# Recurrent layer with gated residual: ScalarE and VectorE held in written order for two steps, the kept steps' transfers pinned to fixed steps

## Chip, cores and metric

The kernel runs on one core of a Trainium2 chip. The metric is the device time in microseconds (us) of one execution, as the median of several. Five engines matter: the PE (TensorE, matrix products), DVE (VectorE), ACT (ScalarE), POOL (GpSimd) and SP (SyncE), which does no arithmetic here and issues nearly all transfers (DMAs) from one queue, in order.

## What is computed

Two layers, in float32, for x of shape 64 × 256 × 1024 (batch, time, width) and a condition of shape 64 × 1024. The second layer's transform is undone by its inverse and the gate is the same for all times, so its result is y · (1 + gate); with the residual it is y · (2 + gate).

```python
# layer 0: a recurrence over 256 time steps, with a residual
xW = einsum('ntd,dh->nth', x, Wx) + b
h  = cond
for t in range(256):
    h = tanh(h @ Wh + xW[:, t])
    y[:, t] = x[:, t] + h
# layer 1: a gate from the condition, on all levels of a Haar transform of y
g    = silu(cond @ W1.T + b1)
gate = sigmoid(g @ W2.T + b2)
out  = y + inverse_haar(gate * haar(y))
```

## The kernel before, in words

**Layout.** A step's state is 64 × 1024; on the chip it is a tile of 128 partitions × 512 elements. The time axis is worked on in pairs of steps: `pairs[i]` holds x for steps 2i and 2i + 1 (128 × 1024), and `s` is the step's place in its pair.

**The recurrent product** h @ Wh (`h_product`, L228) is done by Strassen's scheme in seven quarter-size products, in the order 1, 2, 5, 6, 7, 4, 3. Their left sides come from hT by four DVE operations (`strassen_sides`, L210; L213 to L216), their right sides are Wh's quarters and sums t5, t6, t4 and a changed b12, made once at step 0 (`StrassenWeight`, L150; L164 and L175). Product 1 goes to a PSUM bank m16, ACT copies it out (L236), product 6 is added to it in the same bank and copied again (L240); product 6 can start only after the first copy. Products 2, 3 and 4 are added straight to `acc`, a PSUM bank into which ACT has copied xW of this step before (`put`, L222; L225). DVE joins the parts (L242, L245, L249), ACT does the tanh (L428), DVE the transpose (L430).

**The input product** x @ Wx runs on the same PE in the gaps of the recurrence, one pair ahead. For accuracy x and Wx are split in parts (`XWork`, L265): `x_high` (L116), x1 (L273), x2 (L275) on DVE, and x0, a cast of x_high on ACT (L281). Its `first` part (banks "mixed", then half of "main") is issued in odd steps, its `second` part in even ones. The sums are finished by ACT (L289), POOL (L290) and DVE (L321), written to DRAM (`sum_d`, L325) and read back in the layout of the state (`xw`, eight loads, L331).

**The gate** uses the same PE: the product with W1 at step 0 (tiles `w1_k`), then `gate_hidden` (L387: DVE L388, ACT sigmoid L390, DVE L391 and transpose L393, giving g1T); the product with W2, one block after each of the steps 1 to 8; then `gate_factor` (L396), giving `factor` = 2 + gate.

**Output.** POOL adds hT to the pair (L473) and multiplies by factor (L415); SP stores the pair to yT (L497). For the first four pairs the factor isn't known yet: they are "kept" in DRAM (L500), and each of their eight steps is later loaded again into a tile `again` (L516), multiplied (POOL, L519) and stored (L520). `again` has one buffer (tag "spare", which b1's tile used before), so a load has to wait for the store before it.

**Order of the work.** A scheduler orders each engine's instructions by its own estimate of when they can start, except on engines under `manual_schedule`, which keep the order of the program: PE for the whole kernel, DVE from L355 to `in_order.close()` (L451, behind the split of x for pair 2, in step 0). ACT, POOL and SP are ordered by the scheduler throughout. On each engine the instructions then run strictly in the order so fixed.

**Buffers for W1.** The tag "t" (`sums_tile`, L119) has six buffers, used first by blocks 0 to 5 of Wx, then by blocks of W1, then by t5, t6 and t4 (two tiles each). The pool "slabs" has six buffers, used by pairs of x, blocks 6 and 7 of Wx, the other blocks of W1, and W2.

Of the kernel before, what the change touches and what calls it, by code (L numbers as in the profile page):

```python
# [62 lines left out]
B = D // P  # L63
# [4 lines left out]
KB = B // 2  # L68
S = 2
# [10 lines left out]
def tile_cond_resid(  # L80
# [13 lines left out]
    nc = tc.nc  # L94
    const = ctx.enter_context(tc.tile_pool(name="const", bufs=1))
# [11 lines left out]
    def slab(name: str):  # L107
        return slabs.tile([P, D], F32, tag="slab", name=name)
# [10 lines left out]
    def sums_tile(name: str):  # L119
        return wpool.tile([P, D], F32, tag="t", bufs=3 * KB // 2, name=name)  # L120
# [17 lines left out]
    def load_bias(v: bass.AP, pool, tag: str, name: str):  # L138
        t = pool.tile([P, G, F], F32, tag=tag, name=name)
        for q in range(Q):  # L140
            for g in range(G):
                nc.sync.dma_start(out=t[q * R : (q + 1) * R, g, :], in_=v[q : q + 1, :].broadcast_to((R, F)))
        return t[:].rearrange("p g f -> p (g f)")
# [49 lines left out]
    def plain_product(ps, vT, w, k: int, of=None, start: bool = True, stop: bool = True) -> None:  # L193

        for g in range(G):
            col = of(g) if of else (g * B + k) * R
            for q in range(Q):


                nc.tensor.matmul(  # L200
                    out=ps[q * R : (q + 1) * R, g * F : (g + 1) * F],
                    lhsT=vT[:, col : col + R],
                    rhs=w[:, q * F : (q + 1) * F],
                    start=start and k == 0 and g == 0,
                    stop=stop and k == B - 1,
                    skip_group_check=True,
                    tile_position=(0, q * R),
                )

    def strassen_sides(hT, t: int):  # L210
        a11, a12, a21, a22 = (hT[:, i * E : (i + 1) * E] for i in range(4))
        s = sums.tile([P, 4, E], F32, tag="s", name=f"s{t}")
        nc.vector.tensor_sub(s[:, 2], a11, a21)  # L213
        nc.vector.tensor_add(s[:, 0], a21, a22)
        nc.vector.tensor_sub(s[:, 1], s[:, 0], a11)
        nc.vector.tensor_sub(s[:, 3], a12, s[:, 1])  # L216
        return {1: a11, 2: a12, 3: s[:, 3], 4: a22, 5: s[:, 0], 6: s[:, 1], 7: s[:, 2]}
# [4 lines left out]
    def put(xw, t: int):  # L222

        acc = bank("acc", f"acc{t}")
        nc.scalar.copy(acc, flat(xw))  # L225
        return acc
# [25 lines left out]
    def bank(tag: str, name: str):  # L252
        return one_pool.tile([P, HALF], F32, tag=tag, name=name)
# [86 lines left out]
    h0T = const.tile([P, W], F32, tag="h0T", name="h0T")  # L340
# [11 lines left out]

    ctx.enter_context(tc.manual_schedule(engines={mybir.EngineType.PE}))
    in_order = ExitStack()
    in_order.enter_context(tc.manual_schedule(engines={mybir.EngineType.DVE}))  # L355
    now = XWork(1)
    now.begin()
    acc, acc1, gate_ps = bank("acc", "acc0"), bank("m57", "acc1_raw"), bank("gate", "gate_ps1")
# [8 lines left out]
    w1 = []  # L367

    def load_w1(k: int) -> None:
        w1.append(sums_tile(f"w1_{k}") if k <= KB else slab(f"w1_{k}"))  # L370
        nc.sync.dma_start(out=w1[k], in_=w1T[k])

    def split_block(k: int) -> None:
        wx_s.append(split_weight(wx_raw[k], k))

    for k in range(B):
        x_block(k)
        split_block(k) if k < B - 1 else None
        if k in (3, 5):
            now.block(k // 4)  # L380
    for k in range(KB + 2):
        load_w1(k)
    for k in range(B):
        h_block(k)
# [2 lines left out]
    def gate_hidden(z):  # L387
        nc.vector.tensor_add(z, gate_ps, z)  # L388
        s = work.tile([P, W], F32, tag="h", bufs=1, name="s1")
        nc.scalar.activation(s, z, AF.Sigmoid)  # L390
        nc.vector.tensor_mul(s, s, z)  # L391
        g1T = const.tile([P, W], F32, tag="factor", name="g1T")
        nc.vector.transpose(g1T, s)  # L393
        return g1T

    def gate_factor(z):  # L396
        nc.vector.tensor_add(z, gate_ps, z)
        nc.scalar.activation(z, z, AF.Sigmoid)
        factor = const.tile([P, W], F32, tag="factor", name="factor")
        nc.vector.transpose(factor, z)  # L400
        nc.vector.tensor_scalar_add(factor, factor, 2.0)
        return factor

    def blocks(v):
        return v[:].rearrange("p (g b m) -> p g b m", g=G, b=B)
# [15 lines left out]
    kept, again, factor = [], [], None  # L421
    for t in range(T):
        i, s = divmod(t, S)
        if s == 0 and t:
            xw = xw_next
        if t:
            h = h_product(acc, sides, t)
        nc.scalar.activation(h, h, AF.Tanh)  # L428
        hT = work.tile([P, W], F32, tag="hT", name=f"hT{t}")
        nc.vector.transpose(hT, h)  # L430
        if t + 1 < T:
            sides = strassen_sides(hT, t)
        if t == 0:
            acc = bank("acc", "acc1")
            nc.vector.tensor_add(acc, acc1, b_n)
            split_block(B - 1)
            for k in range(KB + 2, B):
                load_w1(k)
            for k in range(2, B):
                if k == B - 1:  # L440
                    plain_product(gate_ps, h0T, w1[0], 0)
                now.block(k)
            now.take_mixed()
            wh_s = StrassenWeight(wh_raw)
            wh_s.first()
            xw_next = now.finish()
            for k in range(1, B):
                plain_product(gate_ps, h0T, w1[k], k)
            wh_s.others()
            later = XWork(2)  # L450
            in_order.close()  # L451


        elif s == 0:
            acc = put(xw[1], t + 1)
            if i + 1 < NP:
                now.second()
                if i + 2 < NP:
                    later = XWork(i + 2)
                xw_next = now.finish()  # L460
        if s == 1 and i + 2 < NP:
            now = later
            now.first()
        if s == 1 and i + 1 < NP:
            acc = put(xw_next[0], t + 1)

        if t == 1:
            g1T = gate_hidden(b1_n)


        x = pairs[i]
        if t + S < T:
            nc.gpsimd.tensor_add(of_step(x, s), of_step(x, s), blocks(hT))  # L473
        if 1 <= t <= B:
            k = t - 1
            if k == 0:
                gate_ps = bank("gate", "gate_ps2")
            w2 = slab(f"w2_{k}")
            nc.sync.dma_start(out=w2, in_=w2T[k])
            plain_product(gate_ps, g1T, w2, k)  # L480
            if k == B - 1:
                factor = gate_factor(load_bias(b2, const, "h0T", "b2_n"))
        if t + S >= T:

            for half in range(2):
                part = slice(half * KB, (half + 1) * KB)
                v = of_step(x, s)[:, :, part]
                nc.vector.tensor_add(v, v, blocks(hT)[:, :, part])
                nc.vector.tensor_mul(v, v, blocks(factor)[:, :, part])
                to = yT[i].rearrange("p (b s n) -> p s b n", b=B, s=S)[:, s, part]  # L490
                (nc.sync, nc.scalar)[half].dma_start(
                    out=to, in_=x[:].rearrange("p (b s n) -> p s b n", b=B, s=S)[:, s, part]
                )
        elif factor is not None:
            scale(x, s)
            if s == S - 1:
                nc.sync.dma_start(out=yT[i], in_=x)  # L497
        elif s == S - 1:
            kept.append(dram.tile([P, D], F32, tag="kept", bufs=B // S, name=f"kept{i}"))
            nc.sync.dma_start(out=kept[i], in_=x)  # L500
        if s == S - 1:
            del pairs[i]
            if i + 3 < NP:
                load_x(i + 3)


        if t >= 2 * B and t % 2 == 0 and kept:

            def at(v):
                return v.rearrange("p (b s n) -> p s b n", b=B, s=S)[:, r]  # L510

            if t % 4 == 0:
                j, r = divmod(t // 4 - B // 2, S)
                again = const.tile([P, W], F32, tag="spare", name=f"again{t}")
                by_block = again[:].rearrange("p (b n) -> p b n", b=B)
                nc.sync.dma_start(out=by_block, in_=at(kept[j]))  # L516
            else:
                v = again[:].rearrange("p (b g m) -> p g b m", b=B, g=G)
                nc.gpsimd.tensor_mul(v, v, blocks(factor))  # L519
                nc.sync.dma_start(out=at(yT[j]), in_=by_block)  # L520
                if (j + 1, r + 1) == (len(kept), S):
                    kept = []
# [28 lines left out]
```

## Time and profile before

| what | value |
|---|---|
| median of 3 runs | 3113.57 us (3110.15 to 3116.41) |
| span of the profiled execution | 3116.2 us, PE clock 0.996 of full |
| PE busy | 3082.5 us of 3116.2 |
| DVE, ACT, POOL busy | 1757.3, 714.8, 1109.0 us |
| PE waits over 0.1 us, 0 to 262 us | 21.2 us in seven waits |
| PE waits over 0.1 us, 250 to 3080 us | 0.4 us in two waits |
| "again" loads (L516), 8 | issued between 72.9 and 232.5 us |
| "again" products (L519), 8 | between 167.7 and 237.7 us |

The page gives busy times over the whole span. The view of waits lists, for one engine, what it waited for, how long in all and how often. The timeline lists instructions by time; neighbours of one kind are merged ("x32"), and what stands in brackets is the idle time of the engine just before and the instruction that ended it. "SPq" rows are DMA issues on SP's queue; their duration is the issue, not the transfer.

### The profile page before, as it was taken

The page shows a single profiled execution, that of the slowest core. Times are in us where ns is not written, and L with a number is a line of the kernel's source. Part 1 is how long each engine was busy: PE and PEld are TensorE (multiplying, and loading weights), DVE is VectorE, ACT ScalarE, POOL GpSimd, SP SyncE. Part 2 cuts the span into 40 slices and gives each one's busy share as a digit, 9 for nine tenths or more (in the row PEclk, how much of TensorE's full clock was granted, in tenths as well). Part 3 has the DMA queues.
Part 4 walks back from the last instruction along what each step waited for, and adds up shares of the span by engine and source line. Part 5 has one row for each costly group of instructions (what it writes and reads, how often), then busy time and mean ns, then how long its engine had stood idle before and what let it go on. Part 6 is the DMA issues. An engine that isn't in the chain of part 4 may idle for free.

```text
span 3116.2 us, 137774 instructions
## 1 busy us (share of the span) xinstructions
PE 3082.5 (99%) x63856; PEld 2697.4 (87%) x63856; DVE 1757.3 (56%) x2732; ACT 714.8 (23%) x1421; POOL 1109.0 (36%) x766
## 2 busy tenths in 40 slices
PE   8999999999999999999999999999999999999998
PEld 5878888888888888888888888888888888888887
DVE  7555555565555555555655555555555555655554
ACT  3222222222222222222222222222222222222221
POOL 1233333333333333333333333333333333333332
PEclk9999999999999999999999999999999999999999
DMA  7343222222222222222222222222222222222222
GB/s 261 124 120 103 85 92 89 94 86 94 94 90 90 90 91 90 91 90 97 84 93 94 91 86 94 91 91 91 89 94 88 92 89 91 90 91 89 97 71 69
DMA packets 161665, 298.85 MB, mean 96 GB/s; under 512 B 42048, under 2 KB 107840, under 8 KB 161088
## 3 DMA queue, kind: packets, MB, share of 16 engines
q1 hardware_dynamic: 159888, 289.50, 27.3%
q8 instruction: 500, 8.19, 1.1%
q14 instruction: 77, 0.63, 0.1%
q10 hardware_dynamic: 1200, 0.52, 0.1%
HBM read 154.14 MB, written 135.79 MB: 93 GB/s over the span
## 4 chain that ended last, share of the span: by engine, by line
PE 95%; DMA 1%; POOL 0%; DVE 0%; SPq 0%; issue 0%; ACT 0%; DVEq 0%; ACTq 0%; POOLq 0%
PE main L257 30%; PE m L183 29%; PE acc L183 21%; PE mixed L257 15%; DMA again<-kept 1%; DMA yT<-again 0%; POOL again L519 0%; PE gate_ps L200 0%; DMA xw<-sum_d 0%; SPq L331 0%; DVE t L164 0%; DMA x<-xT 0%; DVE h L249 0%; ACT h L428 0%; POOL x L415 0%
## 5 line engine op out<-in xcount | busy, mean ns | idle before, releaser
L473 POOL TENSOR_TENSOR x<-x,hT 128x512 f32<-128x512 f32 x254 | 449.8, 1771 | 1729.2 <-DVE hT L430 1711.7
L257 PE MATMUL main<-wx,x 128*128 128x512 f32 x4064 | 981.1, 393 | 0.0
L257 PEld LDWEIGHTS main<-wx,x 128*128 128x128 f32 x4064 | 752.8, 188 | 178.4 <-issue 25.8
L242 DVE TENSOR_TENSOR y<-m,u 128x256 f32<-128x256 f32 x255 | 108.3, 425 | 882.1 <-PE m L183 882.1
L183 PE MATMUL m<-t,s 128*32 128x128 f32 x16320 | 496.8, 274 | 3.4 <-ACT y L236 3.4
L257 PE MATMUL mixed<-wx,x 128*128 128x512 f32 x2032 | 499.0, 397 | 0.0
L183 PEld LDWEIGHTS m<-t,s 128*32 128x32 f32 x16320 | 454.6, 111 | 4.1 <-ACT y L236 3.6
L257 PEld LDWEIGHTS mixed<-wx,x 128*128 128x128 f32 x2032 | 371.6, 188 | 97.8 <-issue 25.0
L290 POOL TENSOR_TENSOR sum<-sum,b_row 128x512 f32<-128x512 f32 x254 | 326.4, 1286 | 213.0 <-ACT sum L289 213.0
L428 ACT ACTIVATE h<-h 128x512 f32<-128x512 f32 x256 | 162.0, 633 | 790.2 <-DVE h L249 789.0
L415 POOL TENSOR_TENSOR x<-x,factor 128x512 f32<-128x512 f32 x246 | 332.0, 1350 | 15.4 <-DMA x<-xT 5.7
L249 DVE TENSOR_TENSOR h<-acc,y 128x512 f32<-128x512 f32 x255 | 176.4, 692 | 236.4 <-PE acc L183 236.4
L430 DVE STREAM_TRANSPOSE hT<-h 128x512 f32<-128x512 f32 x256 | 182.2, 712 | 204.2 <-ACT h L428 204.2
L183 PEld LDWEIGHTS m<-wh,hT 128*32 128x32 f32 x8160 | 209.0, 110 | 92.8 <-issue 85.6
L275 DVE SCALAR_TENSOR_TENSOR x<-x,x_high 128x1024 fp32r<-128x1024 f32 x127 | 283.9, 2235 | 0.1
L183 PE MATMUL m<-wh,hT 128*32 128x128 f32 x8160 | 276.4, 276 | 4.6 <-DVE hT L430 4.6
L183 PE MATMUL acc<-wh,hT 128*32 128x128 f32 x8160 | 272.2, 274 | 7.2 <-ACT acc L225 7.2
L183 PE MATMUL m<-wh,s 128*32 128x128 f32 x8160 | 270.5, 273 | 0.0
L183 PE MATMUL acc<-wh,s 128*32 128x128 f32 x8160 | 270.3, 273 | 0.2 <-issue 0.2
L183 PE MATMUL acc<-t,hT 128*32 128x128 f32 x8160 | 269.5, 273 | 0.0
L281 ACT CAST x<-x_high 128x1024 fp32r<-128x1024 f32 x127 | 132.9, 1046 | 482.4 <-PE main L257 466.2
L183 PEld LDWEIGHTS acc<-wh,hT 128*32 128x32 f32 x8160 | 229.6, 111 | 8.8 <-ACT acc L225 8.7
(52 smaller groups left out, 2309.1 us busy)
## 6 DMA issues: line engine op xcount, KB each, us to landing
x<-xT SPq DMA_DIRECT2D x128, 512.0 KB, 3.7
sum_d<-sum SPq DMA_DIRECT2D x127, 512.0 KB, 3.1
xw<-sum_d SPq DMA_DIRECT2D x1016, 64.0 KB, 2.0
yT<-x SPq DMA_DIRECT2D x123, 512.0 KB, 3.6
wx<-wx SPq DMA_DIRECT2D x8, 512.0 KB, 8.6
wh<-wh SPq DMA_DIRECT2D x8, 512.0 KB, 11.2
w<-w1T SPq DMA_DIRECT2D x8, 512.0 KB, 8.2
w<-w2T SPq DMA_DIRECT2D x8, 512.0 KB, 4.0
```

What stands on the lines that cost most here:

```text
L183: nc.tensor.matmul(out=out[q * R : (q + 1) * R], lhsT=a[:, k * R : (k + 1) * R], rhs=wh_s.sides[i][k][:, q], start=first and k == 0, stop= ...
L242: nc.vector.tensor_add(y[:, 1:3], m57[:, : 2 * E].rearrange("p (i e) -> p i e", i=2), u[:].unsqueeze(1).broadcast_to((P, 2, E)))
L249: nc.vector.tensor_add(h, acc, flat(y))
L257: nc.tensor.matmul(out=acc[h], lhsT=v[:, k * P : (k + 1) * P], rhs=wx_s[k][which][:, h * HALF : (h + 1) * HALF], start=start and k == 0, s ...
L275: nc.vector.scalar_tensor_tensor(out=self.x2, in0=self.x1[:].bitcast(F32), scalar=-UP, in1=self.high, op0=ALU.mult, op1=ALU.add)
L281: nc.scalar.copy(self.x0, self.high)
L290: nc.gpsimd.tensor_add(s, s, b_row[:, h * HALF : (h + 1) * HALF])
L415: nc.gpsimd.tensor_mul(of_step(x, s), of_step(x, s), blocks(factor))
L428: nc.scalar.activation(h, h, AF.Tanh)
L430: nc.vector.transpose(hT, h)
L473: nc.gpsimd.tensor_add(of_step(x, s), of_step(x, s), blocks(hT))
```

## The change

Four edits. ACT joins DVE in keeping the program's order, and both keep it until behind `gate_hidden` in step 1, where it ended for DVE in step 0. The load of b2 is moved to that place from step 8. Of W1, block 5 goes to a buffer of tag "t" in place of a slab, and block 6 is loaded with the first ones; blocks 0 and 1 of the product with W1, where it was block 0 alone, come ahead of the last x block. The eight kept steps are loaded at the ends of steps 19, 27, ..., 75, where it was steps 16, 20, ..., 44, and multiplied at steps 23, 31, ..., 79; `keep_in_program_order` pins each load on SP, and each product on POOL, behind the instruction that the program has just ahead of it on that engine. The stores L520 are not pinned. The purpose is to keep instructions that the scheduler places early or in a bunch from standing ahead of those that the recurrence needs.

```diff
-    in_order.enter_context(tc.manual_schedule(engines={mybir.EngineType.DVE}))
+    in_order.enter_context(tc.manual_schedule(engines={mybir.EngineType.DVE, mybir.EngineType.Activation}))
...
-        w1.append(sums_tile(f"w1_{k}") if k <= KB else slab(f"w1_{k}"))
+        w1.append(sums_tile(f"w1_{k}") if k < 3 * KB // 2 else slab(f"w1_{k}"))
...
-    for k in range(KB + 2):
+    for k in range(B - 1):
         load_w1(k)
...
-            for k in range(KB + 2, B):
-                load_w1(k)
+            load_w1(B - 1)
             for k in range(2, B):
                 if k == B - 1:
-                    plain_product(gate_ps, h0T, w1[0], 0)
+                    for j in range(2):
+                        plain_product(gate_ps, h0T, w1[j], j)
                 now.block(k)
...
-            for k in range(1, B):
+            for k in range(2, B):
                 plain_product(gate_ps, h0T, w1[k], k)
             wh_s.others()
             later = XWork(2)
-            in_order.close()
...
         if t == 1:
             g1T = gate_hidden(b1_n)
+            b2_n = load_bias(b2, const, "h0T", "b2_n")
+            in_order.close()
...
-                factor = gate_factor(load_bias(b2, const, "h0T", "b2_n"))
+                factor = gate_factor(b2_n)
...
-        if t >= 2 * B and t % 2 == 0 and kept:
+        if t >= 2 * B and t % 4 == 3 and kept:
...
-            if t % 4 == 0:
-                j, r = divmod(t // 4 - B // 2, S)
+            if t % 8 == 3:
+                j, r = divmod(t // 8 - B // 4, S)
...
-                nc.sync.dma_start(out=by_block, in_=at(kept[j]))
+                tc.keep_in_program_order(nc.sync.dma_start(out=by_block, in_=at(kept[j])))
...
-                nc.gpsimd.tensor_mul(v, v, blocks(factor))
+                tc.keep_in_program_order(nc.gpsimd.tensor_mul(v, v, blocks(factor)))
```

## The prediction, made before the changed kernel ran

> **What bounds the kernel now.** I read the page first, for the busiest engine:
>
> ```profile
> PE 3082.5 (99%) x63856; PEld 2697.4 (87%) x63856; DVE 1757.3 (56%) x2732; ACT 714.8 (23%) x1421; POOL 1109.0 (36%) x766
> ```
>
> The core has 33.7 us in which the PE is not busy. The change leaves the count of matmuls alone, so it can win back only PE idle time, and the slow matmuls that follow a pause. The view of waits, PE alone, for 0 to 262 us, says where the idle time is:
>
> ```profile
> PE acc L200 <- DMA wx<-wx: 8.0, 1, 8.0
> PE acc L183 <- ACT acc L225: 7.0, 2, 5.2
> PE m L183 <- ACT y L236: 3.4, 1, 3.4
> PE gate_ps L200 <- issue: 2.4, 1, 2.4
> PE gate_ps L200 <- DMA w<-w1T: 0.4, 2, 0.2
> ```
>
> The same view for 250 to 3080 us shows 0.4 us in all: the steady stretch cannot give anything. The 8.0 us at the start (first weights) and about 5 us at the end (the last two steps) lie outside the edits. Four waits are left, in two places.
>
> Place one, steps 12 and 14 (timeline of PE, SP and ACT; columns: start, us, engine, line, operation):
>
> ```profile
> 193.53 0.61 SPq L325 DMA_DIRECT2D sum_d<-sum  x1
> 199.69 0.57 SPq L520 DMA_DIRECT2D yT<-again  x1
> ...
> 204.15 0.59 ACT L225 COPY acc<-xw 128x512 f32<-128x512 f32 x1 [9.77 <-DMA xw<-sum_d]
> ...
> 204.79 1.94 PE L183 MATMUL acc<-wh,hT 128*32 128x128 f32 x32 [5.23 <-ACT acc L225]
> 206.50 3.64 PE L183 MATMUL m<-t,s 128*32 128x128 f32 x64
> ...
> 233.42 1.08 PE L183 MATMUL acc<-wh,hT 128*32 128x128 f32 x32 [1.80 <-ACT acc L225]
> ```
>
> SP starts its DMAs in one queue. DVE finished sum at 187.5 (L321, 186.84 + 0.69), but sum_d goes out at 193.5, because the queue stood in front of L516, a load of "again" that waits until the previous yT<-again has landed; and the xw loads go out at 200.4, because L520 ahead of them waits for the POOL product L519. So acc is late. The distance between the first matmuls of successive steps, from the PE timeline, is 11.91 us undisturbed; here it is 20.14 for step 12 (198.48 to 218.62) and 13.94 for step 14 (230.54 to 244.48). Excess: 8.23 + 2.03 = **10.3 us**.
>
> Place two, step 1:
>
> ```profile
> 55.29 0.69 DVE L116 TENSOR_SCALAR x_high<-x 128x1024 int32<-128x1024 int32 x1
> 56.01 1.04 ACT L281 CAST x<-x_high 128x1024 fp32r<-128x1024 f32 x1 [11.28 <-DVE x_high L116]
> 56.96 0.26 ACT L236 COPY y<-m 128x128 f32<-128x128 f32 x1
> 57.27 1.93 PE L183 MATMUL m<-t,s 128*32 128x128 f32 x32 [3.38 <-ACT y L236]
> 57.27 1.22 DVE L275 SCALAR_TENSOR_TENSOR x<-x,x_high 128x1024 fp32r<-128x1024 f32 x1
> ...
> 67.66 1.38 DVE L216 TENSOR_TENSOR s<-hT,s 128x128 f32<-128x128 f32 x1
> 68.97 0.68 DVE L391 TENSOR_TENSOR s<-s,b_n 128x512 f32<-128x512 f32 x1
> 69.68 0.71 DVE L393 STREAM_TRANSPOSE g1T<-s 128x512 f32<-128x512 f32 x1
> 70.49 1.89 PE L200 MATMUL gate_ps<-w,g1T 128*32 128x256 f32 x16 [2.38 <-issue]
> ```
>
> The copy of m16 (L236), ready to run at about 52, is queued on ACT behind a cast that waits for DVE. Later the PE waits for g1T, last in DVE's queue. Step 1 with its gate part takes 20.99 us (51.09 to 72.08) and step 2 13.76, where such a step takes 12.82: excess 8.17 + 0.94 = 9.1 us.
>
> [...] after the 5.23 us wait 64 matmuls take 3.64 us, not 1.93; after 1.80 us nothing is slower. But 2.38 us also sufficed (16 matmuls in 1.89, not 1.07). [...] L214 takes 0.29 us alone and 1.38 beside POOL. [...] the trace has 1.28 us ahead of the sigmoid L390.
>
> **The change part by part.**
> *Kept steps pinned.* Now the eight loads L516 run as soon as the buffer is free, so the products L519 and stores L520 crowd between 167 and 240 us. Pinned, a load goes out at the end of steps 19, 27, ... 75, behind the x load, its product four steps later. The buffer's previous store is then four steps (48 us) old, so the load waits for nothing. Queued behind it on SP is the next sum_d: in the steady stretch the x load goes out at 285.00 and sum_d at 295.31, a gap of 10.3 us for an issue of 0.56. The product is 1.28 us on POOL after L415; L290 of that step ends at 282.9 and POOL's next work is at 288.99, a gap of 6 us. The store (0.57 us of SP) then falls before the next sum_d as well. xw lands about 2.6 us before its use (L225 ends 278.55, PE at 281.12), and none of the added transfers (3.1 to 3.5 us each) lies across sum_d or xw. So eight trios cost 0, and both waits go: **−10.3**, bounds −10.3 and −4 if some transfer slips back in front of xw.
>
> *ACT and DVE in written order for steps 0 and 1.* The copy L236 comes ahead of the cast: −3.38 us and the slow matmuls after it, if nothing else holds the PE. But then DVE does. Its order up to x2 (L275) was fixed before as well, and x2 ends at 58.5. PE starts step 1 near 51, needs no x2 for 7 products (about 6.1 us, 57), then waits some 2 us. From x2 on I add rows: L242 0.42, L245 0.29, L249 0.69, tanh 0.63 (0.8 with the gap), transpose 0.71, four sides L213 to L216 of 0.29 to 1.38 (POOL runs L473 and twice L290 beside them, as now: 4.3 in all), L388 0.68, sigmoid 0.63 and gaps, L391 0.68, L393 0.71. That is about 10 us: g1T at 69.1 (59.1 + 10.0; for 59.1 see the W1 blocks), instead of 70.4: −1.3. L388, which now runs early at 58.41, is behind the sides in the new order: behind it wait the sigmoid, L391, L393, and for those the PE. If the table load also comes only after L388, add 1.28: 70.4, as now. The trace of before can't tell, since L388 was long done when the table was loaded. If the sides run beside an idle POOL, take off 2 to 3. I take **−0.7**, midway between the two for the table load; bounds −4 and +2.
>
> *W1 blocks.* Block 5 goes to the last shared buffer, block 6 to the slab that it vacates, so block 6 is loaded up front; the two waits on W1 (0.4 us) should go or stay in part. The product with block 1 comes ahead of x block 7: same PE work, but 16 matmuls (0.89 us) later the mixed sums are finished, so POOL's L290 and DVE's L321 come later, and DVE has been held by them already (0.57 us idle at 47.46). That moves x2 by about +0.6, from 58.5 to 59.1, already counted above. Net **0**, −0.4 to +0.8.
>
> *b2 loaded at step 1*: eight issues of 0.31 us that SP has always made long before step 8. 0.
>
> Sum: −10.3 − 0.7 = −11.0; 3113.57 − 11.0 = **3102.6**.
>
> **The rivals.**
> (a) Step 1 yields more: sides free of POOL, no restart at half rate, −4 to −5 in place of −0.7: about 3098.5 (3113.57 − 10.3 − 4.7). For it: 9.1 us of excess exists. Against: DVE is the engine with a full queue there.
> (b) Pinned transfers still cost something, or step 1 gets slower by the delayed gate: about 4 us of the 11 are left, 3109, not to be told from no change. For it: SP is one queue, and stores L520 are not pinned. Against: the 10 us gap.
> (c) Slower: if all eight stores landed in the queue ahead of xw, as at 199.69 and 227.13, each would cost the mean of the two excesses, 5.1 us: 8 × 5.1 = 41, less the 11.1 won: 3143. Against it: with a ready product the store has nothing to wait for.
>
> **How the numbers follow.** 3102.6: 0.70; (a) 0.13; (b) 0.14; (c) 0.03. The range reaches from below (a), with 2 us for the spread of the runs before (3110 to 3116), to (b): 3096 to 3108.5. Faster by 0.2% means under 3107.3: nearly all of the main case and (a), a tenth of (b): 0.84; same 0.13; slower 0.03.
>
> **What would show it.** Right: steps of 11.91 us from step 9 on without a wait on L225; "again" loads eight steps (95 us) apart; in step 1 no wait on L236, a wait of the PE on x2 in its place, and a first gate product with g1T near 69. Wrong: sum_d or xw issued late behind L516 or L520 at steps 19 to 79; a wait on g1T that ends after 71.

## The result, and the profile after

| | before | after |
|---|---|---|
| median of 20 runs | 3113.1 us (3109.96 to 3116.41) | 3106.66 us (3104.02 to 3108.71) |
| ratio after / before, 95% interval | | 0.9978, [0.9971, 0.9985] |
| span of the profiled execution | 3116.2 us | 3103.8 us |
| first matmul of steps 1, 3 and 9 | 51.09, 85.84, 162.76 us | 49.79, 86.45, 163.37 us |
| steps 12 and 14 | 20.14, 13.94 us | 11.91, 11.91 us |
| steps 1 and 2 | 20.99, 13.76 us | 21.90, 14.76 us |

The kernel became faster by 6.4 us; 11.0 were forecast, with 3096 to 3108.5 as the range. The gain of the pinned transfers came. The small gain forecast for steps 0 to 2 did not: step 3 begins 0.6 us later than before. The ratio, here and below, is estimated by itself from the runs and is not the quotient of the two medians; in the run where they differ most (e1) it means 10.3 us where the medians differ by 8.1.

The PE is busy for 3075.0 us of 3103.8, so 28.8 us are left in which it is not; before they were 33.7. The view of waits, PE alone, 0 to 262 us (what waited, on what; us in total, times, longest):

```profile
PE acc L200 <- DMA wx<-wx: 7.8, 1, 7.8
PE gate_ps L200 <- issue: 6.3, 1, 6.3
PE mixed L257 <- DVE x L275: 0.8, 1, 0.8
PE acc L183 <- issue: 0.6, 1, 0.6
PE gate_ps L200 <- DMA w<-w1T: 0.3, 1, 0.3
```

The two waits on L225 (7.0 us) and the one on the copy L236 (3.4) are gone. The wait on g1T is 6.3 us; it was 2.4. (The view calls it "issue"; the timeline below has the product start 0.11 us after g1T is made.)

**Place one.** What SP's queue waited for at the kept steps, in the whole execution, before (first three lines; 39.7 us together) and after (11.5 us; L517, L520 and L521 are L516, L519 and L520 of before):

```profile
SPq L520 <- POOL again L519: 16.7, 8, 4.7
SPq L520 <- DMA again<-kept: 13.6, 5, 4.1
SPq L516 <- DMA yT<-again: 9.4, 4, 4.1
...
SPq L521 <- POOL again L520: 6.4, 8, 0.8
SPq L517 <- DMA yT<-again: 5.1, 7, 1.8
```

The timeline of SP where a kept step is stored and the next is loaded (step 24):

```profile
344.11 0.36 SPq L498 DMA_DIRECT2D yT<-x  x1
345.34 0.61 SPq L521 DMA_DIRECT2D yT<-again  x1
349.19 0.36 SPq L112 DMA_DIRECT2D x<-xT  x1
349.94 1.46 SPq L517 DMA_DIRECT2D again<-kept  x1
357.73 0.33 SPq L325 DMA_DIRECT2D sum_d<-sum  x1
```

The four ahead of sum_d are through 6 us before sum_d wants the queue. One thing differs from what I had described: the load does not go out four steps after the store, but right behind it. The pin only says "behind the x load that the program has just before it", and that x load runs three to five steps ahead of its place in the program (this one, written for the end of step 27, goes out in step 24). So the load meets its busy buffer after all: SP waits on yT<-again seven times for L517, 5.1 us in all, 1.8 at most. Here it costs nothing, since nothing stands behind it for 6 us.

**Place two.** The timeline of step 1, all engines, in parts:

```profile
50.91 0.27 ACT L236 COPY y<-m 128x128 f32<-128x128 f32 x1 [6.36 <-PE m L183]
57.95 3.92 PE L257 MATMUL mixed<-wx,x 128*128 128x512 f32 x16 [0.84 <-DVE x L275]
61.71 1.98 PE L257 MATMUL main<-wx,x 128*128 128x512 f32 x8
62.38 1.78 DVE L116 TENSOR_SCALAR x_high<-x 128x1024 int32<-128x1024 int32 x1
65.76 0.69 DVE L388 TENSOR_TENSOR b_n<-gate_ps,b_n 128x512 f32<-128x512 f32 x1
66.52 1.28 ACT L390 ACT_TABLE_LOAD   x1 [3.53 <-issue]
67.81 0.63 ACT L390 ACTIVATE s<-b_n 128x512 f32<-128x512 f32 x1
69.20 0.71 DVE L393 STREAM_TRANSPOSE g1T<-s 128x512 f32<-128x512 f32 x1
70.02 1.93 PE L200 MATMUL gate_ps<-w,g1T 128*32 128x256 f32 x16 [6.33 <-issue]
71.69 1.96 PE L183 MATMUL m<-wh,hT 128*32 128x128 f32 x32
```

The copy is in time and the PE has done step 1's x product by 63.7. Then it stands until g1T is made at 69.9. The table of the sigmoid is loaded only when L388 is done, and a split of x for pair 3 (L116), which is outside the fixed order, has slipped in between the sides. (In the trace of before it ran at 59.01, ahead of the sides, in 0.69 us.) After the pause the PE runs at half rate: the granted clock is 0.50 from 68.9 to 75.7 us, and 32 matmuls take 1.96 us, 1.06 otherwise.

### The profile page after: what moved, and what is told of

Same layout as the page of the kernel before. It is cut to its first block, busy times and chain, and to the rows that moved or that the text cites. A ratio compares the mean times of both kernels' runs of the same rounds, so it can differ in the third digit from the quotient of the medians.

```text
span 3103.8 us, 137779 instructions
## 1 busy us (share of the span) xinstructions
PE 3075.0 (99%) x63856; PEld 2691.4 (87%) x63856; DVE 1761.8 (57%) x2732; ACT 716.1 (23%) x1421; POOL 1110.0 (36%) x766
## 4 chain that ended last, share of the span: by engine, by line
PE 97%; DVE 1%; issue 0%; DMA 0%; ACT 0%; SPq 0%; DVEq 0%; ACTq 0%
PE main L257 30%; PE m L183 30%; PE acc L183 21%; PE mixed L257 16%; PE gate_ps L200 0%; DVE t L164 0%; DMA xw<-sum_d 0%; DVE h L249 0%; ACT h L428 0%; DVE hT L430 0%; DVE wh L175 0%; DVE s L215 0%; DVE s L214 0%; DVE x L275 0%; DVE x L273 0%
## 5 line engine op out<-in xcount | busy, mean ns | idle before, releaser
L257 PE MATMUL main<-wx,x 128*128 128x512 f32 x4064 | 981.1, 393 | 0.0
L257 PEld LDWEIGHTS main<-wx,x 128*128 128x128 f32 x4064 | 752.7, 188 | 178.5 <-issue 26.6
L257 PE MATMUL mixed<-wx,x 128*128 128x512 f32 x2032 | 499.0, 397 | 0.8 <-DVE x L275 0.8
L183 PE MATMUL m<-t,s 128*32 128x128 f32 x16320 | 492.7, 273 | 0.2 <-DVE s L215 0.2
L257 PEld LDWEIGHTS mixed<-wx,x 128*128 128x128 f32 x2032 | 371.6, 188 | 98.7 <-issue 24.8
L183 PEld LDWEIGHTS m<-t,s 128*32 128x32 f32 x16320 | 451.0, 110 | 0.5 <-issue 0.5
L290 POOL TENSOR_TENSOR sum<-sum,b_row 128x512 f32<-128x512 f32 x254 | 326.6, 1287 | 202.3 <-ACT sum L289 202.3
L183 PEld LDWEIGHTS m<-wh,hT 128*32 128x32 f32 x8160 | 208.9, 110 | 92.9 <-issue 84.6
L275 DVE SCALAR_TENSOR_TENSOR x<-x,x_high 128x1024 fp32r<-128x1024 f32 x127 | 286.0, 2252 | 0.1
L183 PE MATMUL m<-wh,hT 128*32 128x128 f32 x8160 | 276.3, 276 | 4.6 <-DVE hT L430 4.6
L183 PE MATMUL acc<-wh,hT 128*32 128x128 f32 x8160 | 270.5, 273 | 0.4 <-ACT acc L225 0.4
L183 PE MATMUL acc<-wh,s 128*32 128x128 f32 x8160 | 270.5, 273 | 0.2 <-issue 0.2
L183 PE MATMUL acc<-t,hT 128*32 128x128 f32 x8160 | 269.9, 273 | 0.6 <-issue 0.6
L183 PE MATMUL m<-wh,s 128*32 128x128 f32 x8160 | 269.5, 273 | 0.0
L183 PEld LDWEIGHTS acc<-wh,hT 128*32 128x32 f32 x8160 | 228.5, 110 | 1.2 <-ACT acc L225 1.0
```

The costliest lines, as they stand in the source:

```text
L183: nc.tensor.matmul(out=out[q * R : (q + 1) * R], lhsT=a[:, k * R : (k + 1) * R], rhs=wh_s.sides[i][k][:, q], start=first and k == 0, stop= ...
L257: nc.tensor.matmul(out=acc[h], lhsT=v[:, k * P : (k + 1) * P], rhs=wx_s[k][which][:, h * HALF : (h + 1) * HALF], start=start and k == 0, s ...
L275: nc.vector.scalar_tensor_tensor(out=self.x2, in0=self.x1[:].bitcast(F32), scalar=-UP, in1=self.high, op0=ALU.mult, op1=ALU.add)
L290: nc.gpsimd.tensor_add(s, s, b_row[:, h * HALF : (h + 1) * HALF])
```

## The experiments

Theory: the pins alone make the gain, by keeping SP's queue free ahead of sum_d and xw; the order of ACT and DVE, as given, only moves step 1's wait from the copy to the gate. Rivals: the later places in the program are enough without pins; the order does help, and something else ate the gain; part of the 10.3 us belonged to the one profiled execution. The differences below are those of medians to runs of the kernel before on the same chip (3114.54, 3114.05 and 3114.94 us in the three series); intervals are of the ratio. Runs are called e1 to e11.

### The edits apart

e1_kept_only is the kernel before with this alone (e2_head_only is the changed kernel without it):

```diff
-        if t >= 2 * B and t % 2 == 0 and kept:
+        if t >= 2 * B and t % 4 == 3 and kept:
...
-                nc.sync.dma_start(out=by_block, in_=at(kept[j]))
+                tc.keep_in_program_order(nc.sync.dma_start(out=by_block, in_=at(kept[j])))
...
-                nc.gpsimd.tensor_mul(v, v, blocks(factor))
+                tc.keep_in_program_order(nc.gpsimd.tensor_mul(v, v, blocks(factor)))
```

> The kernel before with the edit on the kept steps alone (later steps, eight apart, pinned); order, W1 and b2 as before. Theory A (the kept steps' queue blocking cost 10.3 us in the trace of before and the pinned version costs nothing): 8 to 10 us faster than before, about 3104, steps 12 and 14 at 11.91 us, step 1 still 21.0 us. Theory B (part of the 10.3 us was particular to the profiled execution, and only some 6 us are there in the median): about 3107, as the whole change measured.

Measured (e1): 3106.43 us, 8.1 faster; ratio 0.9967 [0.9955, 0.9980]. By the difference from before this is the lower end of theory A's 8 to 10 us. Waits of the PE, 0 to 262 us:

```profile
PE acc L200 <- DMA wx<-wx: 8.4, 1, 8.4
PE m L183 <- ACT y L236: 3.8, 1, 3.8
PE gate_ps L200 <- issue: 2.4, 1, 2.4
PE gate_ps L200 <- DMA w<-w1T: 0.2, 1, 0.2
```

Step 1 waits as before, L225 no more. Steps 9 to 80 are 11.91 us each but for step 24, 1.0 over.

> The changed kernel with the kept steps loaded and multiplied as before, so ACT order, W1 and b2 edits alone. Theory A (the head gains nothing: the 3.4 us wait on the copy became a 6.3 us wait on the gate's hidden layer): within 1 us of before, 3112 to 3114. Theory B (the head lost more than its trace shows, which is why the median gained less than 10 us): 3115 or more.

Measured (e2): 3116.41 us, 1.9 slower; ratio 1.0004 [0.9996, 1.0012], which cannot be told from no change. The number is theory B's; the interval leaves A open. SP and PE in its trace:

```profile
220.77 0.55 SPq L517 DMA_DIRECT2D again<-kept  x1
221.76 0.33 SPq L325 DMA_DIRECT2D sum_d<-sum  x1
226.08 0.58 SPq L521 DMA_DIRECT2D yT<-again  x1
226.75 4.01 SPq L331 DMA_DIRECT2D xw<-sum_d  x8
...
231.22 1.94 PE L183 MATMUL acc<-wh,hT 128*32 128x128 f32 x32 [4.57 <-ACT acc L225]
```

The same queue as before the change, with the long wait now in step 14 (7.39 us over) and the short one in step 12 (1.89): 9.3 us together. So the excess is no accident of one execution, though its size is not fixed at 10.3. Step 3 begins at 87.21, 85.84 in the kernel before.

> The changed kernel with ACT left to the scheduler and DVE's fixed order ending in step 0 as before (b2 loaded at step 8); W1 and kept edits stay. Theory A (the fixed order moved the wait and brought nothing): within 1 us of the changed kernel, 3105.5 to 3107.5, step 1 near 21 us with the wait on the copy back. Theory B (the order did help and something else ate it): 2 us or more slower than the changed kernel, 3109.

```diff
-    in_order.enter_context(tc.manual_schedule(engines={mybir.EngineType.DVE, mybir.EngineType.Activation}))
+    in_order.enter_context(tc.manual_schedule(engines={mybir.EngineType.DVE}))
...
             later = XWork(2)
+            in_order.close()
...
             g1T = gate_hidden(b1_n)
-            b2_n = load_bias(b2, const, "h0T", "b2_n")
-            in_order.close()
...
-                factor = gate_factor(b2_n)
+                factor = gate_factor(load_bias(b2, const, "h0T", "b2_n"))
```

Measured (e3): 3106.6 us, 7.9 faster; ratio 0.9971 [0.9960, 0.9981]. Theory A: without the order of ACT the kernel is as fast as with it. Step 1 takes 21.85 us, with 4.2 us on the copy and 2.4 on g1T, 21.90 with the order.

> The changed kernel without the two pins: the kept steps are at the same later places in the program, but the scheduler may move them. Theory A (the pins do it: without them the loads, ready from the start, run as soon as the buffer is free and bunch up again): waits on acc of 5 us and more again between steps 9 and 20, 3113 to 3118. Theory B (the later places in the program are enough): as the changed kernel, 3106 to 3107.

```diff
-                tc.keep_in_program_order(nc.sync.dma_start(out=by_block, in_=at(kept[j])))
+                nc.sync.dma_start(out=by_block, in_=at(kept[j]))
...
-                tc.keep_in_program_order(nc.gpsimd.tensor_mul(v, v, blocks(factor)))
+                nc.gpsimd.tensor_mul(v, v, blocks(factor))
```

Measured (e4): 3116.07 us, 1.5 slower; ratio 1.0004 [0.9996, 1.0012]. Theory A. The rows of its "again" loads, then PE and SP:

```profile
L517 SPq DMA_DIRECT2D again<-kept x8: 542/554/625, 70.4 to 233.6; - x8
...
200.45 0.57 SPq L521 DMA_DIRECT2D yT<-again  x1
201.11 4.01 SPq L331 DMA_DIRECT2D xw<-sum_d  x8
...
205.55 1.94 PE L183 MATMUL acc<-wh,hT 128*32 128x128 f32 x32 [4.53 <-ACT acc L225]
```

Written for steps 19 to 75, the loads ran from 70 to 234 us, as in the kernel before: without pins the later places in the program changed nothing. The pins are the edit that counts. Not tried: pins at the old places, and each of the two pins alone.

### Step 1: what holds g1T

The gate's input is complete when the W1 product ends, near 50 us, yet its hidden layer is computed last. The next run writes it earlier; the sigmoid goes to the gate's PSUM bank. (The diff has the calls in place of the two helper functions that hold them.)

```diff
             later = XWork(2)
+            nc.vector.tensor_add(z, gate_ps, z)              # L388, z is b1_n
+            nc.scalar.activation(gate_ps, z, AF.Sigmoid)
...
         nc.vector.transpose(hT, h)
+        if t == 1:
+            nc.vector.tensor_mul(z, gate_ps, z)
+            nc.vector.transpose(g1T, z)
         if t + 1 < T:
             sides = strassen_sides(hT, t)
```

> The changed kernel with the gate's hidden layer split: its sum and sigmoid written right after the split of x for pair 2 in step 0, its product and transpose between step 1's transpose of h and the four sides (the sigmoid is written to the gate's own PSUM bank). Theory A (the 6.3 us wait of the PE on g1T is a matter of DVE's order alone): g1T ends near 63.5 instead of 69.9, step 1 near 14.7 us and step 2 near 13 us, about 9 us in all: 3097 to 3099. Theory B (the PE would then wait for something else in step 1 or 2, such as the sides): 3103 to 3105, with a new wait on s in step 2.

Measured (e5): 3106.53 us, 7.5 faster than before; ratio 0.9975 [0.9965, 0.9985], not to be told from the changed kernel. Neither theory had the reason, which is in the timeline of ACT and PE:

```profile
58.97 0.60 ACT L389 ACTIVATE gate_ps<-b_n 128x512 f32<-128x512 f32 x1 [10.10 <-DVE b_n L388]
59.51 0.26 ACT L236 COPY y<-m 128x128 f32<-128x128 f32 x1
59.82 1.93 PE L183 MATMUL m<-t,s 128*32 128x128 f32 x32 [5.65 <-ACT y L236]
```

I had rebuilt the fault that the change cures: on an engine in fixed order, an instruction that waits for DVE, ahead of the copy that the PE needs.

> The changed kernel with one small sigmoid (128 x 1) ahead of all else on ACT, so that the sigmoid's table is loaded at the start and never again. Theory A (the table load of 1.28 us lies between L388 and the sigmoid, on the path to g1T): g1T and the first gate product 1.3 us earlier, 3105 to 3105.5. Theory B (the load is hidden): step 1 as in the changed kernel.

```diff
+    one = const.tile([P, 1], F32, tag="one", name="one")
+    nc.vector.memset(one, 0.0)
+    nc.scalar.activation(one, one, AF.Sigmoid)
     now = XWork(1)
```

Measured (e6): 3105.91 us, 8.1 faster than before; ratio 0.9971 [0.9960, 0.9983]; the median cannot be told from the changed kernel's. The trace can:

```profile
66.81 0.69 DVE L391 TENSOR_TENSOR b_n<-gate_ps,b_n 128x512 f32<-128x512 f32 x1
67.59 0.63 ACT L393 ACTIVATE s<-b_n 128x512 f32<-128x512 f32 x1 [2.90 <-issue]
```

(L391 and L393 are L388 and L390 of the changed kernel.) From the end of the sum to the sigmoid 0.09 us instead of 1.36. So the 1.28 us lay on the path to g1T. The table, loaded at 1.18 us, served for the tanh and the copies as well: from 60 to 74 us, with a tanh at 60.49 and copies at 64.09 and 73.49, there is no load. (The traces of before and after have none behind that of the sigmoid, at 65.14 and 66.52, to their ends.) Counted from step 1's first matmul g1T ends at +18.5 us, in the four traces with the same order and the table loaded late at +19.9 on average (18.9 to 20.5): theory A's 1.3 us, though the spread of the four is as large. Counted from the start of the program it ends at 69.7 instead of 69.9, since step 1 began later in this trace.

> The early gate again, with the sigmoid where it can't hold up ACT: DVE's sum L388 stays at the end of step 0, the sigmoid is written in step 1 behind the two copies of m16 and ahead of the tanh. In the run before, the sigmoid, which waits for DVE until 59.0, stood ahead of the copy of m16. Theory A (one order that suits all engines removes both waits of step 1): no wait on the copy, the gate product right after the x product near 64, step 1 near 15 us and step 2 near 13: 7 to 9 us less than the changed kernel, 3098 to 3100. Theory B (DVE holds g1T or the sides back all the same, since the split of x for pair 3 slips in between): step 1 at 16 to 18, 3100 to 3103.

```diff
-            nc.scalar.activation(gate_ps, z, AF.Sigmoid)     # at the end of step 0
...
+        if t == 1:
+            nc.scalar.activation(gate_ps, b1_n, AF.Sigmoid)
         nc.scalar.activation(h, h, AF.Tanh)
```

Measured (e9): 3101.26 us, 13.7 faster than before; ratio 0.9952 [0.9939, 0.9964]. Step 1 takes 15.34 us and step 2 13.15, where the changed kernel has 21.90 and 14.76: 8.2 us. By the steps and by the differences from before (13.7 and 6.4) this is theory A, though the median itself lies in B's range; B's remark is true as well: L116 of pair 3 still came between (62.77, 1.49 us).

> The last kernel with x_high of pair 3 pinned behind step 2's sides on DVE, since the scheduler puts it ahead of step 1's gate or sides. Theory A (it costs DVE 1.5 us on the path to g1T): 1 to 2 us less than the last run. Theory B (it lies in a gap, or its later place delays step 3): no less, or a wait on x2 in step 3.

```diff
-        nc.vector.tensor_scalar(out=t, in0=v.bitcast(I32), scalar1=HIGH, scalar2=None, op0=ALU.bitwise_and)
+        ins = nc.vector.tensor_scalar(out=t, in0=v.bitcast(I32), scalar1=HIGH, scalar2=None, op0=ALU.bitwise_and)
+        if pin:                                              # for pair 3 alone
+            tc.keep_in_program_order(ins)
```

Measured (e10): 3100.20 us, 14.7 faster; ratio 0.9950 [0.9938, 0.9963]. Its DVE, ACT and PE (L390, L431, L395 and L202 are the gate's sum, sigmoid, transpose and product):

```profile
58.17 0.68 DVE L390 TENSOR_TENSOR b_n<-gate_ps,b_n 128x512 f32<-128x512 f32 x1
58.89 0.60 ACT L431 ACTIVATE gate_ps<-b_n 128x512 f32<-128x512 f32 x1 [2.48 <-DVE b_n L390]
62.39 0.71 DVE L395 STREAM_TRANSPOSE g1T<-b_n 128x512 f32<-128x512 f32 x1
63.97 1.07 PE L202 MATMUL gate_ps<-w,g1T 128*32 128x256 f32 x16
```

g1T is ready 0.9 us before the PE comes to it, and the PE doesn't wait. Step 1 is 1.55 us shorter than in the run before, step 2 0.41 longer. The medians of the two, 1.1 us apart, can't be told apart by their intervals.

### The end, and the spread of the runs

In the trace of before the PE waits for hT ahead of each of the last two steps, and then runs slowly:

```profile
3090.39 1.08 PE L183 MATMUL m<-wh,hT 128*32 128x128 f32 x32 [2.28 <-DVE hT L430]
3091.28 1.83 PE L183 MATMUL acc<-wh,hT 128*32 128x128 f32 x32
```

In the trace of after it waits as long (2.28 and 2.34 us) and doesn't slow down: 32 matmuls take 1.06 to 1.08 us. The next run fills the two waits with matmuls that nobody reads.

```diff
+        if t >= T - 2:
+            for j in range(8):
+                nc.tensor.matmul(out=spare, lhsT=w[:, :P], rhs=w[:, :HALF], start=True, stop=True)
         if t:
             h = h_product(acc, sides, t)
```

> The changed kernel with 8 matmuls of 128 x 512 that nobody reads, into a free PSUM bank, ahead of each of the last two steps, in which the PE waits 2.3 us for hT. Theory A (the spread of 4 to 8 us between runs comes in part from those two waits, after which the PE ran at half rate in the trace of before and not in that of after): median 0.5 to 2 us lower, spread of the runs narrower by 1 to 3 us. Theory B (the spread has another origin): median and spread unchanged, or slower by what the 8 matmuls (1.8 us of a 2.3 us wait) do not hide.

Measured (e7): 3104.75 us, 9.3 faster than before; ratio 0.9972 [0.9960, 0.9983]. Median 1.9 lower than the changed kernel's, which the intervals do not separate. Of its six runs, five lie within 1.7 us and one is at 3109.1; on the spread that is inconclusive. The last step begins so:

```profile
3089.30 1.08 PE L183 MATMUL m<-wh,hT 128*32 128x128 f32 x32 [0.30 <-DVE hT L438]
3090.20 1.06 PE L183 MATMUL acc<-wh,hT 128*32 128x128 f32 x32
```

The 13 traces together say more. The last step but one (first matmul to first matmul) takes either 9.1 or 10.3 us, and from the last step's first matmul to the end of the span it is either 13.4 to 13.8 or 15.1 to 15.5. Of the ten kernels without filler, before and after included, five had the long form of the first and eight the long form of the second, with no order in it. The three with filler had the short form of both. So these two waits move an execution by up to 3 us, and in the three traces with filler they did not.

The slowing is in the clock granted to the PE, which the traces record. In that of before it is 0.50 from 3091.40 to 3094.81 us and from 3101.64 to 3105.05, behind waits of 2.28 and 2.35 us; in that of after, behind waits of 2.28 and 2.34, it is 1.00 until the last matmul is done. By the times of their matmuls 13 of the 20 waits (2.28 to 2.36 us) were followed by a slow stretch (32 matmuls in 1.60 to 1.95 us) and 7 were not (1.06 to 1.08). The wait of 2.38 us on g1T in step 1 is alike: behind it 16 matmuls took 1.89 us in before, 1.07 in e1. So at this length the length doesn't decide. What does, no run was made to show. The times go with the clock: of 52 executions of the kernel before, made beside these runs, the 13 with a mean granted clock of 0.998 took 3111.8 us on average, the 18 with 0.997 took 3115.0 and the 21 with 0.996 took 3115.9.

> The three edits of the last runs together: gate's hidden layer early, table first, filler matmuls ahead of the last two steps. Theory A (they act in different places, and the table load is hidden once the gate is early): the sum of early gate and filler, 3095 to 3098, faster than both kernels. Theory B (the first hides the others): as the early gate alone.

Its edits are those shown for e5, e6 and e7. Early gate in its first form, table first and filler together (e8): 3103.91 us, 10.1 faster; ratio 0.9966 [0.9954, 0.9979]. It still had the copy behind the sigmoid (6.6 us on L236), so its theory A could not come true.

> The last kernel with the sigmoid's table loaded first and the 8 filler matmuls ahead of the last two steps. Theory A (the table load of 1.28 us lies on the path from L388 to tanh in step 1, and the filler keeps the end at full rate): 1 to 3 us less than the last run, 3095 to 3098, the fastest of all. Theory B: as the last run.

Its edits are those shown for e5 (with e9's correction), e10, e6 and e7. Measured (e11): 3097.97 us, **17.0 faster than before**, the lowest median of all, though the intervals do not separate it from e10's; ratio 0.9943 [0.9929, 0.9956]; the five runs lie between 3097.15 and 3099.02. Its waits of the PE, 0 to 262 us (L202, L259 and L277 are L200, L257 and L275 of before):

```profile
PE acc L202 <- DMA wx<-wx: 7.9, 1, 7.9
PE mixed L259 <- DVE x L277: 0.6, 1, 0.6
PE gate_ps L202 <- DMA w<-w1T: 0.5, 1, 0.5
PE acc L185 <- issue: 0.5, 1, 0.5
```

The waits on L225, on the copy and on g1T are gone; the first weights' 8 us remain. The table, theory A's first reason, did not bring more here: in e10 it was loaded at 55.12, ahead of the sum, so nothing waited for it.

## Why the prediction was right, and where it was off

**Kept steps pinned, forecast −10.3: right.** There is no wait on L225, and steps 9 to 80 take 11.91 us but for one or two. Alone the edit gave −8.1 by the medians and −10.3 by the ratio, whose interval is −6.2 to −14.0 us. The trace of before held 10.3 us of excess, those of e2 and e4, with the same queue, 9.3 and 9.6; so some 0.8 of the forecast may have been the one execution I had. Step 24 lost 0.6 us in the trace of after, 1.0 in e1 and 1.2 in e11, and nothing in the seven other traces with pins. It need not be a cost of the kept store: in all 13 traces, those without pins included, other single steps are longer by 0.3 to 1.0 us as well (step 212 of before by 0.58, step 178 of e10 by 1.03). The cause stays open. The working had one wrong sentence, "the load waits for nothing": it does wait, as shown, and only the gap on SP, read rightly at 10 us, makes that free.

**ACT and DVE in written order, forecast −0.7: wrong, likely in sign.** The step that failed lies behind g1T: the forecast took it that step 3 moves with g1T. g1T itself came 0.5 us earlier than before, at 69.91 instead of 70.39, near the −0.7, but by errors that cancel. The table load after L388, which I left at half its 1.28 us, is there in full (shown by e6). DVE took in the split of x of 1.78 us that I had not listed, since its order was fixed only for what was written up to the close. Against these, the sides took 3.1 us where I had 4.3, and x2 ended at 57.9 where I had 59.1. The wait on x2, put at 2 us, was 0.8. What I put at nothing is what the slow restart behind g1T adds. From the first gate product to step 3 the PE took 16.43 us instead of 15.35. The rows that differ, before and then after:

```profile
72.08 2.01 PE L183 MATMUL m<-wh,hT 128*32 128x128 f32 x32
73.79 1.20 PE L183 MATMUL acc<-wh,hT 128*32 128x128 f32 x32
74.78 1.96 PE L183 MATMUL m<-t,s 128*32 128x128 f32 x64
...
73.40 1.96 PE L183 MATMUL acc<-wh,hT 128*32 128x128 f32 x32
75.11 2.24 PE L183 MATMUL m<-t,s 128*32 128x128 f32 x64
```

The granted clock says why. In the trace of before it stood at half from 57.0 to 60.4 us, behind the wait on the copy, and from 70.6 to 74.0, behind the wait on g1T. The first lies ahead of g1T, whose time contains what it cost; behind g1T only the second is left. In the trace of after it stood at half once, from 68.9 to 75.7, and all the work in it, 5.7 us, lies behind g1T. The half-rate time is the same, 6.8 us; it has moved to where it delays step 3. In e9 to e11 the longest wait in steps 1 and 2 is 0.9 us, and 32 matmuls of L183 (L185 in e10 and e11) take 1.06 to 1.08 us throughout them.

Step 3 begins at 86.45, 87.21, 87.25 and 86.86 us in the four traces with the order and the table loaded late (after, e2, e4, e7), at 85.84 and 85.38 in the two without edits in the head (before, e1). Means: +1.3 in place of −0.7. But e3, which has the W1 edit with the old order, has 86.72, and the start of step 1 alone differs by up to 1.6 us between these seven traces. So the sign is likely, and how much of the 1.3 us is the order's is not shown.

**W1 blocks, forecast 0: right** as far as it can be seen, though not by the forecast's terms. The two waits on W1 (0.4 us) became one of 0.3 us in the trace of after; in the other ten traces with the edit they are between 0 and 1.5. x2 was to move to 59.1; it ends at 57.9 to 59.3 with the edit, 58.6 on average, and at 58.5 and 58.4 without. The t5 sums (L164) took 2.49 us, not 3.58: in the trace of before one of the four, begun at 44.5 us beside POOL's additions (from 44.31), took 1.77 us and the others 0.68; in that of after each took 0.68, and POOL's additions began at 44.15, 0.3 us before the end of the last.

**b2, forecast 0: right.** The factor's way shows no new wait.

**The sum.** The two edits apart, −8.1 (e1) and +1.9 (e2), make −6.2 by the medians; the whole change measured −6.4. The traces give more: −9.3 to −10.3 for the kept steps and +1.3 for the head make −8.0 to −9.0, within the interval of the ratio (−4.7 to −9.0), but only just; the rest stays open. The two profiled spans differ by 12.4 us; 2.9 of it are the last two steps, which were slow in the one trace and not in the other. The main case, 3102.6, was missed by 4 us, and 3106.66 lies nearer to rival (b)'s 3109; that the result lies in the range is owed to (b), which was there for another reason in its first half. Rival (a) had the right place, the 9 us of excess in steps 1 and 2, and e9 to e11 collected 6 to 7 of them, but not by the order the change gives. Of rival (b) the first half, that pinned transfers still cost something, did not show; the second, "step 1 gets slower by the delayed gate", fits: the late gate and the restart behind it hold up step 3.

The half rate of the PE, by the wait ahead of it: in the timelines read here, waits of 3.38 us (before, step 1) to 8.21 us (e5, first weights) were followed by slow matmuls in all 19 cases, waits of 1.66 to 1.83 us (before, e2, e4, e6) in none of four, and those of 2.28 to 2.38 us in some executions and not in others.

## What to carry to other kernels

When one engine is 99% busy, list its few waits one by one and follow each back through the queue of the engine it waits for: what stood ahead there, and what did that wait for. Fixing an engine's order helps only if the order written is a good one: put an instruction behind everything that another engine needs sooner, and look for what the scheduler may still slip in between. Count what follows the last wait at the rate that the PE will have after it (here 1.96 us for 32 matmuls behind 6.33 us of waiting, 1.06 otherwise). Moving an instruction in the program moves nothing when a scheduler reorders it; pin it, and then check in the trace what the pin is tied to.

## What the runs showed of the hardware

- Pauses of the PE of 2.28 to 2.36 us were followed by half rate in 13 of 20 cases (the last two steps of ten kernels), and not in the other 7; no run was made to show what decides. Half rate there costs 1.2 to 1.7 us each time; two such waits make up to 2.9 of the 5 to 6 us by which 20 runs of one kernel differ.
- The table of the sigmoid can be loaded behind the wait of its instruction (at 66.52, 0.07 us after L388's end, in after) or ahead of it (at 55.12, 3 us before the sum began, in e10); what decides that was not tried. With the sigmoid's table loaded at the start (1.18 us in e6), tanh, sigmoid and copies ran without another load from 60 to 74 us in e6, and from 48 to 88 in e11.
- x_high (L116, 128 x 1024, on DVE) took 0.68 us with POOL idle (54.69 in the trace of after) and 1.78 beside POOL's additions (62.38; L290 from 62.26 to 65.28).
